# Negated softmax maxima: turned by VectorE's 32x32 blocks and sent by small transfers, in place of TensorE transposes and an addition

## The chip, the cores and the metric

The kernel runs on one NeuronCore of a Trainium2 chip. The metric is device time in microseconds of one execution; lower is better. The core has five engines with instruction queues of their own that run side by side and wait for each other through semaphores: TensorE (PE in the profile; its weight loads are listed as PEld), VectorE (DVE), ScalarE (ACT), GpSimd (POOL) and SyncE (SP), which computes nothing and here issues most of the DMA transfers. SBUF is the on-chip memory of 128 partitions; PSUM holds matmul results in 8 banks.

## The reference

The input is x, 4 sequences of 512 tokens with 256 features, all float32. The computation has four parts:

1. Each sequence goes through one gated feed-forward expert out of 8, chosen by the largest entry of its row of `cond_8`.
2. Attention with 16 query heads of 16 features and a single key and value head:

```
q  = (einsum('bte,oe->bto', x, Wq) + bq) * 16**-0.5
k, v = split(einsum('bte,oe->bto', x, Wkv) + bkv)
qr = q.reshape(bsz, NUM_HEADS * tgt_len, HEAD_DIM)       # 8192 query rows
attn_weights = einsum('brd,bsd->brs', qr, k)
attn_probs   = softmax(attn_weights, axis=-1)
attn_output  = einsum('brs,bsd->brd', attn_probs, v)
```

The reshape is a plain one: each token gives 16 query rows. Then an output projection, and x is added.

3. A linear layer whose weight is a sum of 8 masked matrices, mixed by `cond_8`.
4. A mixture of 8 experts with 2 chosen per token and a capacity of 128 per group, added to the result of part 2.

The change touches the softmax of part 2 only. The softmax needs, for every one of 4 x 8192 query rows, the maximum over 512 keys, subtracted before the exponential.

## The kernel before, in words

**Order of the work.** The order of all instructions is written out by hand (`tc.manual_schedule()`): each engine executes its instructions in the order in which the program names them, and SP issues its transfers in that order too. A framework adds the semaphore waits where data or buffers need them. Three stretches follow each other: the conditional expert for all four sequences (0 to some 108 us of the profile), attention with the linear layer and the routing beside it (to about 395 us), and the experts (to the end).

**Attention, units and steps.** A unit `u` is a quarter of a sequence: `b, hg = divmod(u, 4)`; it has 128 tokens by 16 query rows. There are 16 units. Queries lie in `q`, one tile per sequence, two in turn: `[128 partitions, 4 (i), 512 tokens]`. The partitions are four groups (`j`) of 32; in each group rows 0 to 15 hold the 16 features of a query, and rows 16 to 31 are zero. The keys `k` are laid out likewise, four copies in four groups of 32 rows; rows 16 to 31 of each hold ones. So whatever stands in row 16 of a query (`HD` is 16) is added to all its products with the keys. `projection` makes them: `queries(co)` (L316) multiplies, ScalarE writes `stage`, and 8 transfers per call (L327) copy 16 partitions each into q.

The main loop has 64 steps `n` of the exponentials, 4 per unit, and runs the maxima six steps ahead (`LEAD`), `m = n + 6`:

- `maxima(m, js)` (L379): for a block `i` of the unit and each j, a matmul with 128 query rows as weights and 512 keys as the moving operand (L388) into a PSUM bank ("m", 3 of them; in the lead also "x"), and a VectorE reduction that writes the negated maximum of each row (L392) into `negm`, two tiles that take turns by unit.
- `shifted(u)` (L396): when a unit's maxima are complete, four TensorE transposes (L402) turn its `negm` tile, so that each negated maximum comes to partition 32j + 16 of its query's column; VectorE adds q (L406) and writes `qs`, a copy of the unit's queries with the negated maxima in row 16.
- `exponentials(n, js)` (L412): matmuls with 128 keys as weights and the 512 query columns of `qs` as the moving operand (L420), and ScalarE's exponentials (L421). Since row 16 of the keys is one, the product comes out with the maximum subtracted.
- `weigh(n, js)` (L426): the exponentials times the values (L435); the values have a column of ones, which gives the sums. At the end of a unit the result is copied to `stage` and stored in `od` (L445).
- `side(b, k)`: other work, by a table for the step's place k in its sequence: the next sequence's queries in k = 0 and 1, keys and values in 2 and 3; `values` (k = 2) loads the last sequence's results from `od` (L456, L460), `inverse` (k = 3) takes the reciprocal of the sums on VectorE (L485) and sends it out and back (L486, L490), `normalise` follows in k = 5, then output projection, linear layer (k = 6 to 10) and routing.

A step is called in two halves: maxima of two j, exponentials of two j, then weighing or other work. In the steps with `q`, `k`, `v`, `out`, `rT` or `mix` beside them ("dense") the weighing is all in the second half. After the last maxima (from n = 58 on) the steps have exponentials and weighing only.

`shifted(u)` is called when `m % 4 == 1`, two steps after the maxima of the unit's last block: `turning` in the main loop, and `m == 5` in the lead for unit 0. The unit's exponentials begin in the next step.

Of the kernel before, what the change touches and what calls it, by code (L numbers as in the profile page):

```python
# [10 lines left out]
F32 = mybir.dt.float32  # L11
I32 = mybir.dt.int32
AF = mybir.ActivationFunctionType
ALU = mybir.AluOpType
AX = mybir.AxisListType
PSUM = bass.MemoryType.PSUM

P = 128
# [7 lines left out]
HD = 16  # L26
# [15 lines left out]
def adaln_attn_ffn_kernel(  # L42
# [24 lines left out]
    nc = tc.nc  # L67
    mm = nc.tensor.matmul

    const = ctx.enter_context(tc.tile_pool(name="const", bufs=1))  # L70
# [6 lines left out]
    def bank(tag):  # L77
        return ps.tile([P, 512], F32, tag=tag, name=f"ps_{tag}", bufs=BANKS[tag])
# [14 lines left out]
    nil = const.tile([P, 512], F32, name="nil")  # L93
# [36 lines left out]
    qp = attn_ctx.enter_context(tc.tile_pool(name="qp", bufs=2))  # L130
# [67 lines left out]
    ident = const.tile([P, P], F32, name="ident")  # L198
# [39 lines left out]

    negm = []
    for n in range(2):  # L240
        t = const.tile([P, 4, 4, 32], F32, name=f"negm{n}")
        nc.gpsimd.memset(t, 0.0)
        negm.append(t)

    q_tiles = []
    for n in range(2):
        t = const.tile([P, 4, T], F32, name=f"q{n}")
# [3 lines left out]
    def mixed(b, g):  # L251

        c = cond_sb[:, b, g : g + 1]
        w = w2_sb[:, g, :].rearrange("p (c o) -> p c o", c=2)
        wb = wb_sb[:, b, :, 0:D]
        if g == 0:
            nc.vector.tensor_scalar(wb, w, c, None, ALU.mult)
        else:
            nc.vector.scalar_tensor_tensor(wb, w, c, wb, ALU.mult, ALU.add)
# [37 lines left out]


    seqs = [{} for _ in range(B)]
    qs_of = {}  # L300
    e_of = {}
    pa_of = {}
    scatters, last_rows, weighed = [], [], []
# [7 lines left out]
    def project(b):  # L311

        s = seqs[b]
        s["q"] = q_tiles[b % 2]

        def queries(co):  # L316
            def piece():
                pq = bank("x")
                for c in range(2):
                    mm(pq, wq_sb[:, c, ts(co, P)], coT[:, c, ts(b, T)], start=c == 0, stop=c == 1)  # L320
                qd = qp.tile([P, T], F32, name="stage", bufs=4)
                nc.scalar.activation(
                    qd, pq, AF.Identity, bias=bqs_sb[:, co : co + 1], scale=HD**-0.5
                )
                for n in range(2):
                    for j in range(4):
                        nc.sync.dma_start(  # L327
                            s["q"][32 * j : 32 * j + HD, 2 * co + n, :],
                            qd[ds(64 * n + HD * j, HD), :],
                        )  # L330
            return piece

        def keys():
            s["k"] = qp.tile([P, T], F32, name="k")
            pk = bank("x")
            for c in range(2):
                mm(pk, wk_sb[:, c, :], coT[:, c, ts(b, T)], start=c == 0, stop=c == 1)  # L337
            nc.scalar.activation(s["k"], pk, AF.Identity, bias=bk_sb)

        def values():  # L340
            s["v"] = qp.tile([P, 4, 32], F32, name="v")
            pv = bank("x")
            for sc in range(4):
                for c in range(2):
                    mm(  # L345
                        pv[:, ts(sc, 32)], coT[:, c, ds(b * T + sc * P, P)], wv_sb[:, c, :],
                        start=c == 0, stop=c == 1,
                    )
            nc.vector.tensor_tensor(
                s["v"], pv[:, 0:P].rearrange("p (s d) -> p s d", s=4),  # L350
                bv_sb.unsqueeze(1).to_broadcast([P, 4, 32]), ALU.add,
            )

        return {
            "q0": queries(0), "q1": queries(1), "k": keys, "v": values,
        }
# [22 lines left out]
    def maxima(m, js):  # L379

        u, i = divmod(m, 4)
        b, hg = divmod(u, 4)
        q = seqs[b]["q"]
        k = seqs[b]["k"]
        nm = negm[u % 2]
        for j in js:
            pm = bank("x" if len(js) == 4 and j == 3 else "m")
            mm(  # L388
                pm, q[32 * j : 32 * j + 32, i, ts(hg, P)],
                k[32 * j : 32 * j + 32, :], start=True, stop=True,  # L390
            )
            nc.vector.tensor_reduce(  # L392
                nm[:, i, j, HD : HD + 1], pm, AX.X, ALU.max, negate=True
            )

    def shifted(u):  # L396

        b, hg = divmod(u, 4)
        nm = negm[u % 2]
        pt = bank("x")  # L400
        for i in range(4):
            nc.tensor.transpose(  # L402
                pt[:, ts(i, P)], nm[:, i].rearrange("p j d -> p (j d)"), ident
            )
        qs = qp.tile([P, 512], F32, name="qs")
        nc.vector.tensor_tensor(  # L406
            qs.rearrange("p (i t) -> p i t", i=4), pt.rearrange("p (i t) -> p i t", i=4),
            seqs[b]["q"][:, :, ts(hg, P)], ALU.add,
        )
        qs_of[u] = qs  # L410

    def exponentials(n, js):  # L412
        u, sc = divmod(n, 4)
        k = seqs[u // 4]["k"]
        if n not in e_of:
            e_of[n] = ep.tile([P, 4, 4, P], F32, name="e")
        for n4, j in enumerate(js):
            px = bank("m" if n4 >= 2 else "x")
            rows_j = slice(32 * j, 32 * j + 32)
            mm(px, k[rows_j, ts(sc, P)], qs_of[u][rows_j, :], start=True, stop=True)  # L420
            nc.scalar.activation(  # L421
                e_of[n][:, :, j, :].rearrange("p h (i t) -> p i h t", i=4),
                px.rearrange("p (i h t) -> p i h t", i=4, h=4), AF.Exp,
            )

    def weigh(n, js):  # L426

        u, sc = divmod(n, 4)
        b, hg = divmod(u, 4)
        if u not in pa_of:  # L430
            pa_of[u] = bank("a")
        e = e_of[n]
        j0, nj = js[0], len(js)
        for hh in range(4):
            i = mm(  # L435
                pa_of[u][32 * hh : 32 * hh + 32, j0 * P : (j0 + nj) * P], seqs[b]["v"][:, sc, :],
                e[:, hh, j0 : j0 + nj].rearrange("p j n -> p (j n)"),
                start=sc == 0 and j0 > 0, stop=sc == 3 and j0 == 0,
            )
        weighed.append(i)  # L440
        if sc == 3 and j0 == 0:
            o = qp.tile([P, T], F32, name="stage", bufs=4)

            (nc.vector.tensor_copy if u >= 4 * B - 2 else nc.scalar.copy)(o, pa_of[u])  # L444
            (nc.scalar if u == 4 * B - 1 else nc.sync).dma_start(od[b, hg], o)  # L445
# [325 lines left out]
    STEPS = 16 * B  # L771
# [29 lines left out]
    ]  # L801
    for m in range(LEAD):
        maxima(m, (0, 1, 2, 3))
        if m == 5:
            shifted(0)
        for f, b, k in before_steps[m]:
            f(b, k)
        while mixing:
            mixed(*mixing.pop(0))
# [239 lines left out]
    for n in range(STEPS + 1):  # L1049
        m = n + LEAD  # L1050
        if n in (0, 26, 42, 56):
            residual((0, 26, 42, 56).index(n))
        b, k = divmod(n, 16)
        names = [name for _, name in (last if b == B - 1 else beside)[k]] if b < B else []
        dense = (b == 0 and k in behind) or any(
            name.rstrip("0123") in ON_PE and (b > 0 or name in projection[0]) for name in names
        )
        turning = m <= STEPS + 1 and m % 4 == 1
        if m >= STEPS:
            if n < STEPS:  # L1060
                exponentials(n, (0, 1, 2, 3))
            if turning:
                shifted(m // 4 - 1)
            if n == STEPS:

                up(0, 0)
            weigh(n - 1, (2, 3))
            weigh(n - 1, (0, 1))
            if n < STEPS:
                side(b, k)  # L1070
        elif dense:

            maxima(m, (0, 1))
            exponentials(n, (2, 3))
            if turning:
                shifted(m // 4 - 1)
            side(b, k)
            maxima(m, (2, 3))
            exponentials(n, (0, 1))
            if n > 0:  # L1080
                weigh(n - 1, (2, 3))
                weigh(n - 1, (0, 1))
        else:

            maxima(m, (0, 1))
            exponentials(n, (2, 3))
            if n > 0:
                weigh(n - 1, (2, 3))
            maxima(m, (2, 3))
            exponentials(n, (0, 1))  # L1090
            if turning:
                shifted(m // 4 - 1)
            side(b, k)
            if n > 0:
                weigh(n - 1, (0, 1))

    places = itertools.count()

# [154 lines left out]
```

## Time and profile before

| | us |
|---|---|
| median of three timed runs | 688.33 (687.2 to 688.59) |
| the profiled execution, its own time | 676.98 |
| its span, first to last instruction | 675.3 |
| TensorE busy | 656.4 (97%) |
| VectorE busy | 329.6 (49%) |
| ScalarE busy | 225.8 (33%) |
| maxima, reductions (L392) on VectorE | 160.6 + 4.1 |
| transposes of negm (L402) on TensorE | 10.5 |
| addition of q (L406) on VectorE | 10.9 |
| exponentials (L421) on ScalarE | 132.4 + 6.6 |

A line of groups names the source line, the engine, the operation, output and inputs, their shapes, the count, then busy microseconds and mean nanoseconds of one, and last the engine's idle time just before them, with what ended it. A line of the timeline begins with start and duration in microseconds; several alike are merged (x2). A matmul in float32 is listed as two records. Busy times of TensorE overlap: matmuls on different groups of 32 partitions run side by side, and their ends are modelled. SPq is SP's queue: the window of a transfer there is the time to issue it; its landing is listed apart.

### The profile page before, as it was taken

How to read it: one execution, taken by the hardware profiler on the slowest of the kernel's cores; microseconds unless marked ns; L12 is line 12 of the kernel's file. 1: busy time of each engine (PE TensorE's matmuls, PEld its weight loads, DVE VectorE, ACT ScalarE, POOL GpSimd, SP SyncE). 2: the span in 40 equal slices, each digit the busy share in tenths (PEclk: the TensorE clock that was granted, in tenths of full speed). 3: DMA queues.
4: the chain of work that ended last, by engine and by line, in shares of the span. 5: the costliest groups of instructions: out<-in, count | busy, mean ns of one | idle time of the engine just before them, and what ended most of it. 6: DMA issues, size and time to landing. Idle time of an engine off the chain costs nothing.

```text
span 675.3 us, 10833 instructions
## 1 busy us (share of the span) xinstructions
PE 656.4 (97%) x4106; PEld 406.9 (60%) x4106; DVE 329.6 (49%) x782; ACT 225.8 (33%) x400; POOL 118.0 (17%) x149
## 2 busy tenths in 40 slices
PE   8999999999999999999999999999999999999992
PEld 3444433444344433443335368888999999988881
DVE  1174855666667677766897754264222222221110
ACT  1122114555554555455553651222111111121110
POOL 1710000000000000310013041135332222232331
PEclk9999999999999999999999999999999999999997
DMA  6931992100031101330024199537989999975311
GB/s 215 376 108 28 248 259 66 33 17 17 11 96 56 48 17 54 116 103 17 21 85 166 64 323 336 161 106 232 277 255 329 330 323 317 337 235 153 82 22 26
DMA packets 63483, 102.40 MB, mean 152 GB/s; under 512 B 6464, under 2 KB 26560, under 8 KB 63296
## 3 DMA queue, kind: packets, MB, share of 16 engines
q1 hardware_dynamic: 47536, 81.51, 35.7%
q0 software_dynamic: 7008, 10.56, 7.6%
q10 hardware_dynamic: 8880, 9.57, 5.5%
q8 instruction: 34, 0.56, 0.3%
q14 instruction: 25, 0.20, 0.1%
HBM read 75.37 MB, written 24.15 MB: 147 GB/s over the span
## 4 chain that ended last, share of the span: by engine, by line
PE 92%; DVE 3%; DMA 2%; issue 1%; POOL 0%; ACT 0%; SPq 0%; POOLq 0%; DVEq 0%
PE ps_m L983 19%; PE ps_m L388 19%; PE ps_x L1013 17%; PE ps_a L435 9%; PE ps_a L286 4%; PE ps_x L270 4%; PE ps_x L288 4%; PE ps_x L420 3%; PE ps_x L547 2%; PE ps_x L320 2%; PE ps_x L515 2%; PE ps_x L402 1%; DVE negm L392 1%; PE ps_x L337 1%; PE ps_a L968 1%; PE ps_x L345 1%
## 5 line engine op out<-in xcount | busy, mean ns | idle before, releaser
L392 DVE TENSOR_REDUCE negm<-ps_m 128x1 f32<-128x512 f32 x250 | 160.6, 685 | 73.3 <-PE ps_x L420 60.1
L421 ACT ACTIVATE e<-ps_x 128x512 f32<-128x512 f32 x244 | 132.4, 594 | 119.8 <-PE ps_x L420 115.9
L388 PE MATMUL ps_m<-k,q 32*128 32x512 f32 x500 | 150.4, 639 | 0.1
L420 PE MATMUL ps_x<-qs,k 32*128 32x512 f32 x488 | 139.9, 639 | 0.0
L983 PE MATMUL ps_m<-xT,wi_sb 128*128 128x128 f32 (+1 forms) x800 | 130.3, 321 | 0.0
L1013 PE MATMUL ps_x<-wo_sb,e 128*128 128x256 f32 x576 | 128.5, 379 | 0.0
L983 PEld LDWEIGHTS ps_m<-xT,wi_sb 128*128 128x128 f32 x800 | 119.0, 191 | 10.1 <-issue 0.4
L1013 PEld LDWEIGHTS ps_x<-wo_sb,e 128*128 128x128 f32 x576 | 107.6, 190 | 13.7
L987 ACT ACTIVATE e<-ps_m 128x512 f32<-128x512 f32 x72 | 42.8, 597 | 194.1 <-PE ps_m L983 192.6
L1024 POOL DMA_INDIRECT out_dram<-y,to_row x36 | 56.1, 1558 | 140.5 <-DMA out_dram<-y,to_row 74.4
L388 PEld LDWEIGHTS ps_m<-k,q 32*128 32x128 f32 x500 | 44.6, 183 | 54.3 <-issue 23.9
L435 PE MATMUL ps_a<-e,v 128*32 128x256 f32 x1024 | 73.7, 387 | 1.4 <-ACT stage L444 1.0
L435 PEld LDWEIGHTS ps_a<-e,v 128*32 128x32 f32 x1024 | 24.2, 108 | 70.6 <-issue 54.4
L970 DVE COPY xT<-ps_a 128x256 f32<-128x256 f32 (+1 forms) x23 | 12.2, 529 | 95.1 <-PE ps_a L968 95.1
L1023 DVE TENSOR_SCALAR y<-ps_x,w 128x256 f32<-128x256 f32 x36 | 17.4, 482 | 81.2 <-PE ps_x L1013 81.2
L665 POOL DMA_INDIRECT xp<-x,to_i x32 | 33.2, 1038 | 57.7 <-DVE negm L392 34.1
L420 PEld LDWEIGHTS ps_x<-qs,k 32*128 32x128 f32 x488 | 38.6, 183 | 3.3 <-issue 2.6
L597 POOL TENSOR_SCALAR x<-mk 128x4 f32<-128x4 f32 x4 | 0.8, 210 | 219.6 <-DVE mk L594 219.5
L291 DVE SCALAR_TENSOR_TENSOR hid<-ps_x,wo_sb,sg 128x512 f32<-128x512 f32 x16 | 12.0, 749 | 47.1 <-PE ps_x L288 44.1
L286 PE MATMUL ps_a<-xT_sb,wi_sb 128*128 128x512 f32 x64 | 30.5, 598 | 0.9 <-DMA wi_sb<-in_wcond_dram 0.9
L288 PE MATMUL ps_x<-xT_sb,wi_sb 128*128 128x512 f32 x64 | 30.1, 592 | 0.0
L270 PE MATMUL ps_x<-hid,wo_sb 128*128 128x512 f32 x64 | 28.7, 595 | 0.0
(155 smaller groups left out, 472.6 us busy)
## 6 DMA issues: line engine op xcount, KB each, us to landing
wi_sb<-in_wi_dram SPq DMA_DIRECT2D x25, 1024.0 KB, 8.1
wo_sb<-in_wo_dram SPq DMA_DIRECT2D x25, 1024.0 KB, 8.0
xp<-zeros ACTq DMA_DIRECT2D x1, 8580.0 KB
od<-stage SPq DMA_DIRECT2D x15, 256.0 KB, 2.1
wi_sb<-in_wcond_dram SPq DMA_DIRECT2D x12, 256.0 KB, 5.8
xt<-xp SPq DMA_DIRECT2D x11, 260.0 KB, 5.9
xT_sb<-in_xT_dram SPq DMA_DIRECT2D x4, 512.0 KB, 7.7
w_sb<-in_w_dram SPq DMA_DIRECT2D x8, 256.0 KB, 5.2
```

The source lines that it names most:

```text
L270: mm(po, wd[:, hc, ts(dc, P)], hid_of[b][:, hc, :], start=hc == 0, stop=hc == 3)
L286: mm(pu, wu[:, c, :], xT_sb[:, c, ts(b, T)], start=c == 0, stop=c == 1)
L288: mm(pg, wg[:, c, :], xT_sb[:, c, ts(b, T)], start=c == 0, stop=c == 1)
L388: mm(pm, q[32 * j : 32 * j + 32, i, ts(hg, P)], k[32 * j : 32 * j + 32, :], start=True, stop=True,)
L392: nc.vector.tensor_reduce(nm[:, i, j, HD : HD + 1], pm, AX.X, ALU.max, negate=True)
L420: mm(px, k[rows_j, ts(sc, P)], qs_of[u][rows_j, :], start=True, stop=True)
L421: nc.scalar.activation(e_of[n][:, :, j, :].rearrange("p h (i t) -> p i h t", i=4), px.rearrange("p (i h t) -> p i h t", i=4, h=4), AF.Exp,)
L435: i = mm(pa_of[u][32 * hh : 32 * hh + 32, j0 * P : (j0 + nj) * P], seqs[b]["v"][:, sc, :], e[:, hh, j0 : j0 + nj].rearrange("p j n -> p (j ...
L983: mm(ph[:, ts(k, n)], wi_of[u][:, c, ts(f0 + k, P)], xT_of[u][:, c, :], start=c == 0, stop=c == 1,)
L987: nc.scalar.activation(hT_of[u][:, f0 : f0 + each].rearrange("p f t -> p (f t)"), ph, AF.Gelu_apprx_tanh,)
L1013: mm(po[:, 0:D], hT_of[u][:, fc, ts(h, P)], wo_of[u][:, fc, :], start=fc == 0, stop=fc == F // P - 1,)
L1024: i = nc.gpsimd.indirect_dma_start(out=out_rows, out_offset=bass.IndirectOffsetOnAxis(ap=to, axis=0), in_=y, in_offset=None, compute_op=AL ...
```

## The change

Four edits, all around `shifted`:

- The maxima are kept closer: `negm` becomes `[128, 4 (i), 32]`, with j in the first 4 of 32 columns.
- `shifted(u)` is now one VectorE transpose of 128x128, which turns each block of 32x32 by itself, into `nmT`, and four SP transfers. Each takes 4 partitions (one for each j), for each of them 4 runs (i) of 32 elements, and writes them to row 16 of the four groups of the query tile itself. There is no `qs`; the exponentials read q directly, as 4 runs of 128 columns.
- Row 16 of a query tile then holds old maxima when the tile is used again (sequences 2 and 3). `queries` therefore sends zeros from `nil` into that row first, two more transfers per call.
- `shifted(u)` is called at once after the unit's last maxima: at the end of the step with `m % 4 == 3` (steps n = 1, 5, 9, ...), and at `m == 3` for unit 0. On SP's queue its transfers come behind the query transfers of places 0 and 1 and ahead of the loads of `values` in place 2.

```diff
-        t = const.tile([P, 4, 4, 32], F32, name=f"negm{n}")
+        t = const.tile([P, 4, 32], F32, name=f"negm{n}")
...
                 for n in range(2):
+                    if b > 1:
+                        nc.sync.dma_start(s["q"][HD:P:32, 2 * co + n, :], nil[0:4, :])
                     for j in range(4):
...
-                nm[:, i, j, HD : HD + 1], pm, AX.X, ALU.max, negate=True
+                nm[:, i, j : j + 1], pm, AX.X, ALU.max, negate=True
...
     def shifted(u):
         b, hg = divmod(u, 4)
-        nm = negm[u % 2]
-        pt = bank("x")
-        for i in range(4):
-            nc.tensor.transpose(
-                pt[:, ts(i, P)], nm[:, i].rearrange("p j d -> p (j d)"), ident
-            )
-        qs = qp.tile([P, 512], F32, name="qs")
-        nc.vector.tensor_tensor(
-            qs.rearrange("p (i t) -> p i t", i=4), pt.rearrange("p (i t) -> p i t", i=4),
-            seqs[b]["q"][:, :, ts(hg, P)], ALU.add,
-        )
-        qs_of[u] = qs
+        nmT = qp.tile([P, 4, 32], F32, name="nmT")
+        nc.vector.transpose(
+            nmT.rearrange("p i t -> p (i t)"), negm[u % 2].rearrange("p i j -> p (i j)")
+        )
+        for a in range(4):
+            nc.sync.dma_start(
+                seqs[b]["q"][HD:P:32, :, ds(hg * P + 32 * a, 32)],
+                nmT[32 * a : 32 * a + 4],
+            )
...
-            mm(px, k[rows_j, ts(sc, P)], qs_of[u][rows_j, :], start=True, stop=True)
+            mm(
+                px, k[rows_j, ts(sc, P)], seqs[u // 4]["q"][rows_j, :, ts(u % 4, P)],
+                start=True, stop=True,
+            )
...
-        if m == 5:
+        if m == 3:
             shifted(0)
...
-        turning = m <= STEPS + 1 and m % 4 == 1
...
-            if turning:
-                shifted(m // 4 - 1)
...
+        if m < STEPS and m % 4 == 3:
+            shifted(m // 4)
```

The lines with `turning` stand in all three branches of the main loop and go from each.

More of the change, by code (lines that the diff above doesn't have):

```diff
@@ L299, in adaln_attn_ffn_kernel @@
     seqs = [{} for _ in range(B)]
-    qs_of = {}
     e_of = {}
@@ L1074, in adaln_attn_ffn_kernel @@
             exponentials(n, (2, 3))
-            if turning:
-                shifted(m // 4 - 1)
             side(b, k)
@@ L1090, in adaln_attn_ffn_kernel @@
             exponentials(n, (0, 1))
-            if turning:
-                shifted(m // 4 - 1)
             side(b, k)
```

## The prediction

> **What bounds the kernel now.** I read the page first (busy shares, slices, the chain that ended last), then the groups by shape, then the instruction timeline of the attention stretch (108 to 394 us) and SP's own timeline. The page's chain by engine:
>
> ```profile
> PE 92%; DVE 3%; DMA 2%; issue 1%; POOL 0%; ACT 0%; SPq 0%; POOLq 0%; DVEq 0%
> ```
>
> The groups that the change removes (count, then busy us and mean ns, then idle before):
>
> ```profile
> L406 DVE TENSOR_TENSOR qs<-ps_x,q 128x512 f32<-128x512 f32 x16 | 10.9, 682 | 0.3 <-PE ps_x L402 0.3
> ...
> L402 PE MATMUL ps_x<-ident,negm 128*128 128x128 f32 x64 | 10.5, 286 | 0.0
> ```
>
> TensorE carries the chain, and L402 has 1.4% of it by line: 9.5 us of 675.3. What one turning is worth depends on the step. I call the stretch from one pair of maxima to the next a half step. TensorE's timeline at unit 7 (step 27):
>
> ```profile
> 307.64 0.70 PE L388 MATMUL ps_m<-k,q 32*128 32x512 f32 x2
> ...
> 309.28 0.96 PE L388 MATMUL ps_m<-k,q 32*128 32x512 f32 x2
> ...
> 310.61 0.66 PE L402 MATMUL ps_x<-ident,negm 128*128 128x128 f32 x4
> 311.20 0.64 PE L435 MATMUL ps_a<-e,v 128*32 128x256 f32 x8
> 311.77 1.13 PE L388 MATMUL ps_m<-k,q 32*128 32x512 f32 x4
> ...
> 314.10 0.70 PE L388 MATMUL ps_m<-k,q 32*128 32x512 f32 x2
> ```
>
> Ordinary halves alternate 1.64 and 1.90 us; with the turning they take 2.49 (309.28 to 311.77) and 2.33. So one turning costs 1.28 us here: 0.59 of TensorE, the rest because the 0.68 us addition delays VectorE's maxima, which free the three "m" banks. In steps dense with projections TensorE runs back to back, VectorE idles 0.3 to 0.8 us a half, and a turning costs only its 0.49 us.
>
> SP matters too. Its timeline where queries and attention outputs meet (steps 16 to 19):
>
> ```profile
> 181.41 4.94 SPq L327 DMA_DIRECT2D q<-stage  x8
> 186.45 0.53 SPq L445 DMA_DIRECT2D od<-stage  x1
> 187.07 5.54 SPq L327 DMA_DIRECT2D q<-stage  x8
> 192.67 0.58 SPq L456 DMA_DIRECT2D sum<-od  x1
> 193.30 1.34 SPq L460 DMA_DIRECT2D o<-od  x2
> 197.03 0.33 SPq L486 DMA_DIRECT2D ivd<-iv  x1
> ```
>
> SP is solid from 181.4 to 194.6: about 0.62 us per issue. VectorE's reciprocal of these sums follows, without a wait today:
>
> ```profile
> 196.25 0.29 DVE L349 TENSOR_TENSOR v<-ps_x,bv_sb 128x128 f32<-128x128 f32 x1 [0.43 <-PE ps_x L345]
> 196.46 0.54 DVE L485 RECIPROCAL iv<-sum 128x64 f32<-128x64 f32 x1
> ...
> 197.30 1.29 DVE L392 TENSOR_REDUCE negm<-ps_m 128x1 f32<-128x512 f32 x2 [0.30 <-PE ps_x L420]
> ```
>
> **What the Trainium skill says.** "DMA: Bandwidth & Descriptors", Anatomy of one DMA: a fixed cost of about 2.0 us, mostly completion, whatever the size. The trace agrees: 1.9 us to landing for q<-stage, 2.1 for sum<-od. "Perfetto Trace Analysis", Per-instruction lifecycle: the profiled window of a DMA instruction is sequencer and descriptor generation, not the movement. So the 0.62 us is SP's time, and small size need not make it shorter; the trace has 0.32 to 0.34 us for lone issues and 0.5 to 0.7 back to back. The same page, Identifying Dependency Chains: an instruction waiting on several engines gets EventSemaphore instructions ahead of it. The trace shows them at 51 ns each on TensorE's queue. "VectorE: DVE Perf Modes", The three transpose paths: 311 ns for a 128x128 bf16 turn in 32x32 blocks. No run here shows it.
>
> **Part by part.**
>
> *Removed: 64 transposes, 16 additions.* Units 0 to 3, 5, 6, 9, 10 and 14 fall in dense steps: 9 x 0.49 = 4.4 us. Units 7 and 11: 1.28 each, 2.6. Units 4, 8, 12 and 13 also have other VectorE work around them; there I count 0.58 for the transposes and the excess of the next half (3.40 against 2.99, or 2.00 against 1.64): 0.95 each, 3.8. Unit 15 is priced below as a whole. Gain 10.8 us. One "x" bank per unit falls free too, counted at nothing: it was taken where TensorE waited anyway.
>
> *Added on VectorE: 16 turns.* I take 0.31 us; bounds 0.19 (a 128x32 operation here) and 0.68 (the addition). They come after a step's last maximum, ahead of the next half's reductions, where VectorE waits 0.35 to 0.8 us for TensorE, so nearly all is hidden. Without that cover 16 x 0.31 = 5.0. I take 0.6, for the steps with routing work.
>
> *Waits on TensorE.* The first exponential matmul of each unit waits on four transfers, up to four EventSemaphores: 0 to 0.2 us x 16, so 0 to 3.2. TensorE's queue usually runs ahead, and the maxima that wait on a query transfer and VectorE show no longer half (2.06). I take 0.6. The moving operand becomes four 128-element runs of q; no row shows such a matmul, I count nothing (bounds 0 and a few us).
>
> *Added on SP: 64 transfers of 2 KB, and 8 zero fills for the last two sequences.* Usually SP is idle and they are covered: unit 4's maxima end near 169.6, plus turn and four issues and 1.9 us lands near 174, against exponentials at 176 or later. Three places differ. Let c be SP's time per small issue; I take 0.62, as q<-stage, bounds 0.33 (lone) and 1.1 (the longest q<-stage is 1139 ns).
>
> Unit 5 (step 17) and unit 9 (step 33). The turned maxima are queued behind both query sets, and the sums behind them. The first zero fill issues early, since it waits only for old exponentials; three fills and four turned transfers remain ahead of sum<-od: 7c. In unit 5 the sums land at 192.67 + 2.1 + 7c. The reciprocal could start at 196.05 (end of v, 0.49 earlier than before). VectorE is in order: behind the reciprocal wait the maxima of the next two positions, behind these the "m" banks and TensorE. About 0.6 us of slack (0.30 idle before the reductions, some 0.3 until the bank is asked for) comes off: 7c - 1.9 = 2.5 us. In unit 9 sum<-od issued at 267.43 and v ended at 272.61: 7c - 3.2 = 1.1. The exponentials, which need the turned maxima by about 197.7 in unit 5, are hidden behind this stall or late by less. Unit 1 also comes after 16 query transfers (they end at 122.38), but lands by 125.7 against 127.1, no loss.
>
> Unit 15 (step 57). The following steps have no maxima and are short, and in VectorE's queue the turn stands behind the last sequence's first ranking, which ends with L595 at 380.34. Turn 0.31, semaphore 0.1, so first issue at 380.75, last at + 3c, landing 1.9 later: 384.5. TensorE's exponentials of step 60 start today at 383.44:
>
> ```profile
> 380.15 0.19 DVE L595 TENSOR_TENSOR hot<-rev,mk 128x32 f32<-128x32 f32 x1
> ...
> 381.26 0.66 PE L402 MATMUL ps_x<-ident,negm 128*128 128x128 f32 x4
> ...
> 383.44 0.70 PE L420 MATMUL ps_x<-qs,k 32*128 32x512 f32 x2
> ```
>
> So a loss of 3c - 0.8 = 1.1 us, its own saved transposes included.
>
> *Smaller negm fills* on POOL are early and hidden. From 395 us on TensorE runs the experts without a break (265.00 busy of 265 in that window), and their loads and rows follow the earlier work, so the gain passes to the end.
>
> Sum: -10.8 + 0.6 + 0.6 + 2.5 + 1.1 + 1.1 = -4.9 us. The profiled execution would go from 676.98 to 672.1. The timed median is 688.33, 11.4 above it, a difference that the profile doesn't explain; I carry the same 4.9 over: **683.4 us**.
>
> **Rivals.**
>
> *Full cover.* SP issues these tiny transfers in 0.33 us. Unit 5 then loses 0.4, unit 9 nothing, unit 15 0.2: -10.8 + 1.2 + 0.6 = -9.0, 679.3 us. For it: lone issues take that. Against: everything back to back takes 0.5 or more.
>
> *Slower: SP becomes the bound in steps 16 to 19 and 32 to 35 and at unit 15.* Each transfer has 16 runs of 128 bytes; if c is 1.1, the three places lose 5.8, 4.5 and 2.5, and -9.6 + 12.8 = +3.2: 691.5 us. It decides above c = 0.91 (17c = 9.6 + 1.9 + 3.2 + 0.8). For it: the longest query issue; against: their median, 587 ns.
>
> *Landing late everywhere.* If four runs of 128 bytes per partition landed 2 to 3 us later than the 1.9 of the query transfers, the spare of ordinary units would be gone and fifteen exponentials would wait; 0.5 us each takes 7.5 us and gives about 691 once the three places grow as well. Nothing in the profile says so: DMA engines are under 30% busy there, and 32 KB lands in 1.9.
>
> *Hardly any gain:* the hidden waits on TensorE (3.2) or VectorE (5.0) show in full: 686 to 687.
>
> **How the numbers follow.** Forecast 0.52; full cover 0.17; hardly any gain 0.12; slow SP 0.12; late landing 0.07. A change of this kernel can be told from none at about 0.2%, 1.4 us. Faster: 0.52 + 0.17 and half of "hardly any", 0.75; same 0.08; slower 0.17. The range 678.8 to 690.2 leaves out the ends of full cover and of both slow cases. The likeliest case alone: 681 to 686.
>
> **What would show it.** Halves at 311.77 and its like back to 1.64 and 1.90; no L402 or L406. SP solid from the query transfers to sum<-od, 4.3 us later than before relative to the first of them, and VectorE idle before the reciprocal in steps 19 and 35, released by a DMA. TensorE idle about 1 us before step 60, released by the q transfers. I am wrong if small issues take clearly other than 0.62 us, if other exponentials wait on q transfers, or if exponential matmuls last longer than 0.59 to 0.70 us.

## The result, and the profile after

| | before, us | after, us | ratio, 95% interval |
|---|---|---|---|
| first measurement | 688.31 | 692.19 | 1.0065 (1.0048 to 1.0082) |
| chip 12, later | 677.46 | 673.14 | 0.9935 (0.9918 to 0.9951) |
| chip 0, later | 687.68 | 692.25 | 1.0060 (1.0039 to 1.0080) |

The measurement that the prediction was made for says 0.65% slower, and 692.2 lies outside the forecast's range. The other two rows came with the experiments: the chips on which these kernels ran fall into two kinds. On chips 9, 12 and 13 the kernel before takes 677.5 to 677.6 us, on chips 0 and 11 (and in the first measurement) 687.2 to 688.3, each time within a few tenths of a per cent. I call these the shorter and the longer level. Only chip 0 was met twice, both times at the longer level, so the runs don't tell the chip from the time at which it ran. The profile of before that the prediction was made from (676.98 us) is of the shorter level, the times beside it are of the longer one.

Of the profile after, first the chain by engine:

```profile
PE 87%; DVE 3%; DMA 3%; SPq 2%; another core or an unknown queue 1%; ACT 1%; issue 1%; POOL 0%; POOLq 0%; DVEq 0%
```

TensorE still carries it, but with 87% in place of 92%. New are SP's queue and a releaser that the profile cannot name. L402 and L406 are gone; in their place stands (count, then busy us and mean ns, then idle before):

```profile
L403 DVE STREAM_TRANSPOSE nmT<-negm 128x128 f32<-128x128 f32 x16 | 4.9, 306 | 0.4
```

TensorE's timeline at unit 7, where the prediction showed halves of 1.64, 2.49 and 2.33 us (start, duration, count at the end):

```profile
311.13 0.70 PE L391 MATMUL ps_m<-k,q 32*128 32x512 f32 x2
...
312.77 0.96 PE L391 MATMUL ps_m<-k,q 32*128 32x512 f32 x2
...
314.67 0.70 PE L391 MATMUL ps_m<-k,q 32*128 32x512 f32 x2
...
316.52 0.74 PE L391 MATMUL ps_m<-k,q 32*128 32x512 f32 x2
```

They are 1.64, 1.90 and 1.85 now: the gain is there. Next SP's timeline and what waits for it in unit 5:

```profile
188.35 3.33 SPq L330 DMA_DIRECT2D q<-stage  x4
191.79 2.40 SPq L407 DMA_DIRECT2D q<-nmT  x4
194.23 0.56 SPq L459 DMA_DIRECT2D sum<-od  x1
```

```profile
196.41 0.55 DVE L488 RECIPROCAL iv<-sum 128x64 f32<-128x64 f32 x1 [3.15 <-DMA sum<-od]
196.88 2.53 DVE L395 TENSOR_REDUCE negm<-ps_m 128x1 f32<-128x512 f32 x4
197.56 0.69 PE L391 MATMUL ps_m<-k,q 32*128 32x512 f32 x1 [1.50 <-DVE negm L395]
```

The four transfers stand ahead of the sums, at 0.60 us each; the reciprocal waits 3.15 us for the sums, the maxima stand behind it, and TensorE waits for the banks that these free. That is the step which the prediction priced at 2.5 us. What it did not price comes next. In this view of windows, PEclk is the third value from the end:

```profile
197.00:199.00 2.00, 1.44 (x10) 0.67 (x14) 1.98 (x4) 0.10 (x1) 0.00 (x0) 1.00 0.53 193
199.00:201.00 2.00, 2.00 (x16) 0.52 (x8) 0.41 (x1) 0.99 (x2) 0.00 (x0) 0.57 0.16 53
201.00:203.00 2.00, 2.00 (x16) 0.58 (x16) 1.29 (x2) 1.34 (x3) 0.00 (x0) 0.58 0.31 104
```

For some 3.4 us after the stall TensorE runs at half its clock, and the next half takes 3.03 us for 1.90.

Three more stalls, near 291, 363 and 396 us, had no place in the prediction at all. The timeline of all engines at the first:

```profile
289.18 0.97 POOL L668 DMA_INDIRECT xp<-x,to_i  x1 [0.30 <-issue]
289.66 1.12 PE L391 MATMUL ps_m<-k,q 32*128 32x512 f32 x2
291.82 1.29 DVE L395 TENSOR_REDUCE negm<-ps_m 128x1 f32<-128x512 f32 x2 [4.77 <-PE ps_m L391]
291.96 1.08 ACT L424 ACTIVATE e<-ps_x 128x512 f32<-128x512 f32 x2 [3.91 <-PE ps_m L391]
292.56 0.69 PE L391 MATMUL ps_m<-k,q 32*128 32x512 f32 x1 [1.78 <-DVE negm L395]
```

VectorE and ScalarE stand still for 4 to 5 us while GpSimd issues the last two of eight indirect scatters of routed rows (L668); TensorE runs on until it needs a bank, and then waits for VectorE. VectorE's wait is put down to a matmul of TensorE that ended 4.0 us before (why it was not seen earlier is taken up below, where the scatters are moved); in the same stretch at the shorter level VectorE never idles over 0.8 us (timeline below). The half that begins at 289.66 takes 5.73 us, where it takes 2.07 at the shorter level.

### The profile page after: what moved, and what is told of

Read it like the earlier page. It is cut to its first block, busy times and chain, and to the rows that moved or that the text cites. A ratio compares the mean times of both kernels' runs of the same rounds, so it can differ in the third digit from the quotient of the medians.

```text
span 690.5 us, 10751 instructions
## 1 busy us (share of the span) xinstructions
PE 660.7 (96%) x4042; PEld 403.1 (58%) x4042; DVE 324.0 (47%) x782; ACT 226.0 (33%) x400; POOL 116.1 (17%) x149
## 4 chain that ended last, share of the span: by engine, by line
PE 87%; DVE 3%; DMA 3%; SPq 2%; another core or an unknown queue 1%; ACT 1%; issue 1%; POOL 0%; POOLq 0%; DVEq 0%
PE ps_m L986 18%; PE ps_m L391 18%; PE ps_x L1016 17%; PE ps_a L438 8%; PE ps_a L287 4%; PE ps_x L271 4%; PE ps_x L289 4%; PE ps_x L550 2%; PE ps_x L320 2%; PE ps_x L518 2%; PE ps_x L420 2%; DVE negm L395 2%; PE ps_a L971 1%; SPq L407 1%
## 5 line engine op out<-in xcount | busy, mean ns | idle before, releaser
L391 PE MATMUL ps_m<-k,q 32*128 32x512 f32 x500 | 157.2, 651 | 5.6 <-DVE negm L395 5.5
L420 PE MATMUL ps_x<-q,k 32*128 32x512 f32 x488 | 143.6, 654 | 3.5 <-DVE xT L973 2.2
L986 PE MATMUL ps_m<-xT,wi_sb 128*128 128x128 f32 (+1 forms) x800 | 131.7, 323 | 0.0
L391 PEld LDWEIGHTS ps_m<-k,q 32*128 32x128 f32 x500 | 46.4, 186 | 63.5 <-DVE negm L395 35.5
L438 PE MATMUL ps_a<-e,v 128*32 128x256 f32 x1024 | 76.3, 395 | 3.1 <-issue 2.0
L420 PEld LDWEIGHTS ps_x<-q,k 32*128 32x128 f32 x488 | 38.7, 186 | 7.7 <-issue 4.4
L668 POOL DMA_INDIRECT xp<-x,to_i x32 | 32.1, 1004 | 57.2 <-DVE negm L395 34.3
L1024 POOL CAST to_row<-at 128x1 int32<-128x1 f32 x36 | 19.8, 551 | 66.0 <-DVE at L1009 66.0
```

Of the source, the lines that this page charges most:

```text
L391: mm(pm, q[32 * j : 32 * j + 32, i, ts(hg, P)], k[32 * j : 32 * j + 32, :], start=True, stop=True,)
L420: mm(px, k[rows_j, ts(sc, P)], seqs[u // 4]["q"][rows_j, :, ts(u % 4, P)], start=True, stop=True,)
L438: i = mm(pa_of[u][32 * hh : 32 * hh + 32, j0 * P : (j0 + nj) * P], seqs[b]["v"][:, sc, :], e[:, hh, j0 : j0 + nj].rearrange("p j n -> p (j ...
L668: i = nc.gpsimd.indirect_dma_start(out=xp, out_offset=bass.IndirectOffsetOnAxis(ap=to_i[:, k, ch : ch + 1], axis=0), in_=s["x3"][:, ch, 0: ...
L986: mm(ph[:, ts(k, n)], wi_of[u][:, c, ts(f0 + k, P)], xT_of[u][:, c, :], start=c == 0, stop=c == 1,)
```

## Experiments

Halves are counted as in the prediction, from one pair of maxima to the next. All runs stand beside the kernel before on the same chip.

**The two kernels again (chip 12, shorter level).**

> The kernel before, unchanged, for a second profile of it. Theory A (the 677.0 us profile of before is an execution without stalls, and a usual one holds about 11 us of them): timed 688.3, ratio 1.000, and this profile shows about 688 with stretches of all compute engines idle for 2 to 7 us, each followed by some 3 to 10 us of TensorE at a clock of 0.5. Rival B (the 11 us lie outside what the profile sees, or come from the profiling): a profile at 677 again, TensorE clock 0.994 again, and 688.3 timed.

> The changed kernel again: 692.2 timed. If the three long stalls of its first profile (at 291, 363 and 395 us, about 5, 4 and 12 us with the half clock behind them) belong to the program, they come back at the same instructions, and the profile is again near 692. If they are chance, they are elsewhere or gone, and the profile differs from 692 by several us.

Before: 677.36 us, ratio 0.9999 (0.9990 to 1.0008). After: 673.14, 0.9935 (0.9918 to 0.9951). The profile of after at the place of the first long stall:

```profile
290.55 0.70 PE L391 MATMUL ps_m<-k,q 32*128 32x512 f32 x2
...
291.70 1.29 DVE L395 TENSOR_REDUCE negm<-ps_m 128x1 f32<-128x512 f32 x2 [0.63 <-PE ps_x L420]
...
292.62 0.70 PE L391 MATMUL ps_m<-k,q 32*128 32x512 f32 x2
```

A half of 2.07 us, with scatters in flight up to 291; the stalls near 363 and 396 are gone as well. The stall of unit 5 is there (halves of 5.10 and 2.43 us). So the sum of the prediction holds where its profile was taken: 677.4 to 673.1 is 4.3 us of the 4.9 forecast. Theory A (before's profile was untypical for its place) and rival B (the profile sees nothing) both miss: it is typical, for this level.

**SP's queue: sums ahead of the turned maxima.**

```diff
-        if m < STEPS and m % 4 == 3:
+        if m < STEPS and m % 4 == 3 and m // 4 not in (5, 9):
             shifted(m // 4)
+        if m in (24, 40):
+            shifted(m // 4 - 1)
```

> The changed kernel, but units 5 and 9 are turned and sent one step later, behind the loads of the attention sums on SP's queue. Theory A: the stalls at the reciprocal of steps 19 and 35 go, 3.0 of 4.0 us and 1.0 of 1.2 (three zero fills stay ahead of the sums): 692.2 - 4.0 = 688.2. Rival D (the exponentials of these units, which then wait for transfers that start about 4 us later, take over the wait): 691 to 692.

675.99 us (chip 12), 0.9970 of before (0.9957 to 0.9983), 2.9 us slower than the changed kernel. That is rival D, and worse than it said:

```profile
192.73 1.29 SPq L463 DMA_DIRECT2D o<-od  x2
194.13 2.35 SPq L407 DMA_DIRECT2D q<-nmT  x4
194.27 0.55 DVE L488 RECIPROCAL iv<-sum 128x64 f32<-128x64 f32 x1 [0.69 <-DMA sum<-od]
...
198.97 2.07 PE L420 MATMUL ps_x<-q,k 32*128 32x512 f32 x4 [2.42 <-DMA q<-nmT]
```

The reciprocal's wait falls to 0.69 us, and TensorE waits 2.42 us for the transfers instead. Both waits come of what stands ahead on the queue: the 16 query transfers, and here also the two loads of o, 256 KB each, which the edit puts ahead of the turned maxima. From 194.1 to 197.0 us the DMA engines move 226 packets, only 8 of them under 512 bytes; the 64 packets of 128 bytes that are the turned maxima move from 197.0 to 198.0. The clock is then halved for 6.8 us.

**The changed kernel, without transfers, and with SP's queue relieved (chip 0, longer level).** The second kernel leaves out transfers and fills, so its exponentials have no shift (they are scaled by 0.004 to stay finite). The third:

```diff
     beside = [
...
-        [(1, "q1"), (-2, "rank1")],
+        [(1, "v"), (-2, "rank1")],
         [(-1, "values"), (1, "k"), (-2, "places"), (-2, "rows")],
-        [(1, "v"), (-1, "inv")],
+        [(-1, "inv"), (1, "q1")],
...
             exponentials(n, (0, 1))
+            if m == STEPS - 1:
+                shifted(m // 4)
             side(b, k)
...
-        if m < STEPS and m % 4 == 3:
+        if m < STEPS - 1 and m % 4 == 3:
             shifted(m // 4)
```

> The changed kernel once more, beside the kernel before in the same call, since the first measurement (before 688.3, after 692.2) and the second (before 677.5, after 673.1) differ. Theory E (what decides is where the kernels run: on some chips or at some times both hold extra stalls): the kernel before is either near 677.5 and the changed one near 673, or near 688 and 692, and in the second case the profile shows long stalls while GpSimd issues its indirect scatters. Rival F (chance in each execution): values of one call are spread over both levels.

> The changed kernel without the 64 transfers and the 8 zero fills, VectorE's turns kept; so that the exponentials stay finite without their shift they are scaled by 0.004, and the values that come out are others, so that the routing differs. If the transfers cost only what units 5, 9 and 15 show (5.10+2.43 against 1.64+1.90 us, then 3.38+1.64 against 2.07+1.64, and 4.77 against about 3.35), this runs 4.0 + 1.3 + 1.4 = 6.7 us below the changed kernel: 666.4 where that takes 673.1. If the transfers slow anything else (DMA queues, instruction fetches), it is lower still, or the long stalls of the first measurement go with them.

> The changed kernel with the second half of the query projection and the value projection of the next sequence exchanged (queries in the fourth step instead of the second), so that only 8 query transfers stand ahead of the turned maxima of units 1, 5 and 9 and of the attention sums, and with unit 15 turned and sent ahead of the last routing instead of behind it. My theory (SP's queue makes the stalls): units 5, 9 and 15 lose at most 0.3 us each, and it runs near 666.5 to 667.5 where the changed kernel takes 673.1, 1.5% under the kernel before. Rival (the stalls move to the query transfers, which now stand behind the reciprocal and its round trip): 670 or more.

Before 687.68; after 692.25, 1.0060 (1.0039 to 1.0080): the first measurement repeats, with its stalls at the same halves (7.11 and 3.66 us, 5.75 and 3.34, 5.48), as theory E has it. Without transfers 677.87, 0.9853; with the queue relieved 681.19, 0.9887 (0.9839 to 0.9934). Both still have long stalls (a half of 7.26 us at the second set in the latter), so their totals mix two things, and the totals named in the expectations, for the shorter level, aren't tested. Up to the half where unit 9's reciprocal comes, no scatter is in play; from the first maxima (72 us) to there, the kernel before takes 195.9 us, after 192.2 here (194.5 on chip 12), relieved 190.5, without transfers 190.1. So with the queue relieved the transfers cost 0.4 us up to there, and the rest is unit 5. The relieved kernel at units 5 and 15:

```profile
195.12 0.70 PE L391 MATMUL ps_m<-k,q 32*128 32x512 f32 x2
...
196.79 0.92 PE L391 MATMUL ps_m<-k,q 32*128 32x512 f32 x2
...
377.20 0.31 DVE L403 STREAM_TRANSPOSE nmT<-negm 128x128 f32<-128x128 f32 x1
377.59 2.41 SPq L407 DMA_DIRECT2D q<-nmT  x4
...
382.22 0.70 PE L420 MATMUL ps_x<-q,k 32*128 32x512 f32 x2
```

Halves of 1.67 and 1.87 us in unit 5; in unit 15 the half ahead of step 60 is 3.53 (3.94 before, 4.76 after). The part of my theory that concerns SP is shown.

**Spreading the scatters, first try (chip 9, then chip 0).** The scatters were moved to later steps in the order in which the program is written:

```diff
-            for ch in range(4):
-                for k in range(2):
-                    i = nc.gpsimd.indirect_dma_start(
+                bursts = ((1,) * 8, (3, 3, 2), (2, 2, 2, 2), (8,))[b]
...
+    for part in range(1, 8):
+        beside[4 + part].append((-2, f"scatter{part}"))
```

> The kernel before, for a profile where it takes near 688 (if this call meets that level; at 677 it repeats the earlier profile). Theory G (where a kernel takes the longer time, VectorE and ScalarE stand still while GpSimd issues its indirect scatters of routed rows, until the last scatter of a set of eight is through; each such stall of TensorE is followed by 3 to 10 us at half its clock): the 10 to 11 us of before lie in the same three sets, in halves that begin near 291, 360 and 390 us. Rival H (the extra time of before lies elsewhere, and the stalls at the scatters belong to the changed kernel): these halves are as in its first profile (2.07, 2.54 and 2.08 us).

> The changed kernel with its indirect scatters spread out: the first sequence's eight go one to a step over eight steps, the second's as three, three and two over three steps, the third's as four pairs over four steps, in place of eight in a row each. Theory G: where the changed kernel takes 692 (19 us above its 673), a stall lasts only while one short burst is in flight, and most of the 19 us go: 674 to 682; where it takes 673, nothing changes, 672.5 to 674. Rival (the stalls don't hang on the scatters, but on the place in the program): 690 to 693, with the long halves near 288, 361 and 393 us as before.

> The same spread scatters together with the exchanged projections and the early turn of unit 15 (681.2 without the spread where before took 687.7). Theory G: 667 to 674 at the longer level, 666 to 667 at the shorter. Rival: 681 at the longer level.

Chip 9 has the shorter level: before 677.47 (0.9999), after with this edit 673.97, 0.9936 (0.9915 to 0.9957), and with the queue relieved 668.61, 0.9869 (0.9852 to 0.9885).

> Again for a profile of the kernel before at its longer level, which the third call (677.6) did not meet. Theory G (VectorE and ScalarE stand still while a set of eight indirect scatters is in flight, and TensorE's clock halves after each): its 10 to 11 us lie in the halves near 291, 361 and 390 us. Rival H: these are 2.07, 2.54 and 2.08 us as in its first profile, and the time is elsewhere. If the call meets the shorter level: 677.5 and nothing new.

> Changed kernel with spread scatters, at the longer level if the call meets it. Theory G: 674 to 682 (against 692.2 for the changed kernel there). Rival (the place in the program decides): 690 to 693. At the shorter level it repeats 674.0.

> Exchanged projections, early turn of unit 15 and spread scatters, at the longer level if the call meets it. Theory G: 667 to 674 (681.2 without the spread). Rival: 681. At the shorter level it repeats 668.6.

Chip 0, longer level: 687.42 (1.0005), 689.48 (1.0050, 1.0029 to 1.0072), 682.12 (0.9909, 0.9879 to 0.9939). The spread runs seem to speak for the place in the program, but the trace shows that nothing was spread: GpSimd has no other work between, is bound to no step, and issues its eight scatters 1.28 us apart as ever. The edit tested nothing.

The profile of before at the longer level is worth more. Its span is 685.8 us against 675.6 on chip 12. Summed over the halves around each set of scatters, it loses 1.8 us at the first set, 1.1 at the second and, from there into the experts (to 440 us), 7.2 at the third: 10.1 of these 10.2. Rival H falls: the extra time of before lies at the scatters too. The third set, windows of chip 12 and then of chip 0 (PE busy, PEld, DVE, ACT, POOL, PEclk, DMA share, GB/s):

```profile
396.00:400.00 4.00, 4.00 (x33) 2.85 (x32) 0.97 (x2) 2.37 (x3) 2.18 (x3) 1.00 1.05 406
400.00:404.00 4.00, 4.00 (x20) 3.52 (x20) 3.58 (x2) 1.19 (x2) 0.00 (x0) 1.00 1.04 407
```

```profile
396.00:400.00 4.00, 1.63 (x4) 0.29 (x2) 0.28 (x1) 1.75 (x3) 3.02 (x4) 0.94 0.88 335
400.00:404.00 4.00, 3.78 (x18) 1.48 (x19) 0.00 (x0) 1.58 (x5) 0.95 (x1) 0.50 1.04 410
```

On chip 0 TensorE is busy 1.63 us of four while GpSimd issues three scatters and starts another, and then has half its clock. The same count for the changed kernel (chip 0 against chip 12) gives 6.3 us at the first set, 3.4 at the second and 11.0 at the third; it reaches the first set 2.8 us earlier there, 2.2 of it because unit 5 cost less, and 6.3 + 3.4 + 11.0 - 2.8 = 17.9, the whole difference of the spans (690.5 and 672.6).

**Do the stalls follow the scatters? (chip 11, longer level).** One kernel holds the first set back to step 42. The other truly spreads it, one scatter a step, each waiting for TensorE; its second and third sets, though bound to steps, still went out nearly in a row, since they were late already. Both add to the scatters:

```diff
+                    tc.add_manual_dep(
+                        i.ins, weighed[-1].ins.name, AFTER, reason="not at once"
+                    )
```

> The changed kernel with the first sequence's eight scatters held back from step 36 to step 42 (each waits for TensorE's last weighing of that step), the other sets as they are. Theory G, at the longer level: the halves near 288 us, where the changed kernel lost 5.0 and 1.5 us, are clean (3.0, 2.1, 2.1 us), and either the time falls to about 686 or a stall comes up where the scatters now are, near 305 to 318 us. Rival I (the place in the program decides, scatters or not): the halves near 288 us stay at 5 to 7 us, and 690 to 693. At the shorter level: 673, nothing to see.

> The changed kernel with its scatters truly spread: the first spread edit only moved them in the order in which the program is written, and GpSimd, which has nothing between them, still issued them in a row. Here each burst waits for TensorE's last weighing of its step: one a step over eight steps, then three, three and two over three, then four pairs. Theory G, at the longer level: a stall lasts at most until one short burst is through, 674 to 684. Rival I: 689 to 693. At the shorter level: 673 to 674.

> The truly spread scatters with the exchanged projections and the early turn of unit 15. Theory G, at the longer level: 667 to 675 (681 and 682 without true spreading). Rival I: 680 to 684. At the shorter level: 667 to 669.

Before 687.89; moved 697.62, 1.0135 (1.0118 to 1.0151); spread 682.24, 0.9911 (0.9893 to 0.9929); spread and relieved 677.94, 0.9853 (0.9830 to 0.9875). With the set moved, the halves near 290 us are clean (2.07, 2.13, 2.36), and the timeline has this where the scatters now are:

```profile
308.87 1.12 PE L391 MATMUL ps_m<-k,q 32*128 32x512 f32 x2
...
312.12 0.97 POOL L675 DMA_INDIRECT xp<-x,to_i  x1 [0.31 <-issue]
314.92 1.89 DVE L395 TENSOR_REDUCE negm<-ps_m 128x1 f32<-128x512 f32 x3 [7.32 <-remote]
315.07 1.08 ACT L424 ACTIVATE e<-ps_x 128x512 f32<-128x512 f32 x2 [7.58 <-remote]
315.67 1.22 PE L391 MATMUL ps_m<-k,q 32*128 32x512 f32 x1 [5.68 <-DVE negm L395]
```

The half at 308.87 takes 9.82 us for 1.90. The stall follows the scatters: rival I falls. VectorE comes back 2.80 us after GpSimd began the last of the eight, as it does in the other profiles: 2.64 in the first profile after, 2.59 on chip 0, 1.96 in before.

What is late is a signal. VectorE's maxima and ScalarE's exponentials wait for one semaphore, which TensorE raises when matmuls end, and the trace keeps a record of each update. In the changed kernel on chip 0, eight matmuls that raise it end between 284.80 and 288.84 us. No update is recorded from 283.92 to 289.78 us, and then eight within 0.33 us; VectorE starts at 289.85 and ScalarE at 289.99. On chip 12 each update of that stretch follows the end of its matmul within 0.15 us, and in none of the ten profiles of the shorter level does one come more than 0.6 us late. So TensorE's signals don't arrive while the row of scatters is in flight, and the two engines that wait for them stand still. ("remote" in the lines above names an update for which the view finds no instruction that ended shortly before.) Some records are missing in the traces of the longer level (849 of 860 for this semaphore on chip 0), but in the first set all eight are there. What holds the signals up isn't shown. The packets of the scatters themselves aren't slower: in the first set they take 123 ns each, on the mean, on chip 0 and on chip 12.

With the set spread (three in a row, then 4.5 to 6.8 us apart) the halves near 291 are clean too (2.08, 2.13, 2.36), while the second set, in a row, costs a half of 7.78 us. So the row stalls; scatters 4.5 us or more apart did not.

**All three sets handed out singly (met the shorter level, chip 13).** One scatter at each step or weighing, the experts' first loads two steps later for it:

```diff
         weighed.append(i)
+        if held and (n < 48 and j0 == 0 or n >= 48):
+            f, nth = held.pop(0)
+            f(nth)
...
-        [(-1, "rT0"), (-1, "rT1"), (0, "pairs1")],
+        [(-1, "rT0"), (-1, "rT1")],
...
-        [(-1, "choose"), (-1, "rank0")],
+        [(0, "pairs1"), (-1, "choose"), (-1, "rank0")],
```

> The kernel before with the scatters of the first three sequences handed to GpSimd one at a time, each waiting for a weighing of TensorE: the first set one a step, the second and third one at each weighing (about 2 us apart); the first weights of the experts are loaded two steps later for it. If rows of scatters make the stalls, then at the longer level this falls from 688 by most of the 10 to 11 us: 677 to 682. Rival (2 us apart is as bad as 1.3): the first set's 1.6 us go, the rest stays: 686. At the shorter level 677 to 678.

> The same handing out in the changed kernel. If rows of scatters make its 19 us of stalls: 673 to 678 at the longer level, 4 us under the kernel before with the same edit, as the sum and the shorter level have it. Rival: 682 as with the first spreading, the second and third sets still stalling. At the shorter level 673.

> The same handing out, with the exchanged projections and the early turn of unit 15: 667 to 672 at the longer level (rival: 676 to 678, as with the first spreading), 667 to 669 at the shorter.

680.20 (1.0036, 1.0026 to 1.0047), 676.13 (0.9980, 0.9964 to 0.9996) and 671.98 (0.9916, 0.9900 to 0.9933), beside 677.58. The edit itself costs 2 to 3.4 us there (the half ahead of step 60 grows from 3.94 to 8.82 in before, from 4.77 to 7.87 in after); between the two kernels the 4.1 us stay. What it does at the longer level wasn't met.

## Why the prediction was wrong

**The step that failed** is the one from profile to time: "The timed median is 688.33, 11.4 above it, a difference that the profile doesn't explain; I carry the same 4.9 over". The profile was of the shorter level, where the sum is nearly right (4.3 for 4.9 us). The 11 us are stalls at three sets of scatters (10.1 of the 10.2 us that the profiles of before differ by), and they do not carry over: in the changed kernel they are 20.7, or 10.6 more, of which 2.8 come back ahead of the first set. In the four profiled executions, 3.0 us won at the shorter level (675.6 to 672.6) become 4.7 lost at the longer one (685.8 to 690.5); in the medians, 4.3 won become 3.9 and 4.6 lost. I had seen the gap, and named it as unexplained; what follows from an unexplained 11 us in a forecast of 5 is that it can change with the kernel, which was none of my rivals.

Why the changed kernel loses more is partly seen. The stall ends with its set, so its length is set by where in the set VectorE and ScalarE run out of signals. In before, at the first set, VectorE comes to a stop 0.4 us after the last scatter began; in the changed kernel (chip 0) 2.2 us ahead of it, with two still to come, and in the moved set 4.5 us ahead of it. What decides that point isn't shown. Late instruction fetches could be thought of: in the changed kernel on chip 0 no packet of an instruction queue moves between 282.7 and 294 us, around a stop from 285.1 to 289.9. But the fetch that comes at 294.2 us there comes at 291.0 on chip 12, where that stretch is reached 2.8 us later. It is late by 6.0 us, about what the stall costs, so it can be a result of the stall as well as a cause.

**Removed work: right.** 9.6 us of gain net of turns and waits were forecast outside units 5, 9 and 15. In the halves of chip 12, leaving out those of units 5, 9 and 15 and the stretches around the first two sets, it is 8.4; those stretches (0.4 and 0.6) and unit 9's own transposes (0.4) bring it to 9.8. A dense unit gained 0.39 to 0.44 for the 0.49 forecast, unit 7 1.07 for 1.28. The turn took 0.31 us, what the Trainium skill ("VectorE: DVE Perf Modes", The three transpose paths) has for elements of half the size, and exponential matmuls kept 0.59 to 0.70 us with their moving operand in four runs.

**Issue time c: right.** 0.54 to 0.60 us for 0.62; the fills 0.54.

**Unit 5: right in mechanism, one term missing.** Priced 2.5, measured 1.9 and 2.2 (chip 0), 3.1 (chip 9), 4.1 (chips 12 and 13), 4.0 (first profile), 4.3 and 5.5 (chip 11). Two things make the spread. The reciprocal waits 2.2 us where no query transfer takes over 0.9 us to issue (chips 0 and 9), and 2.9 to 3.2 us where one of them takes 1.4 to 1.5. And on chip 0 there is no half clock behind the stall, elsewhere there is, for 3.4 us (6.8 in the case of 5.5), which the prediction has no term for. "TensorE: Matmul & The Clock Gate" in the skill (Part 1) has windows of 3413 ns that run free, and half rate after an idle one; the length agrees. Windows that run free could also let like stalls end differently: the reciprocal waits 2.18 us on chip 0 and 2.19 on chip 9, and only the second halves the clock. But TensorE idled 0.5 to 1.5 us in these stalls, far less than a whole window, so what halves the clock here stays open.

**Unit 9: right** (1.1 forecast; 1.3 in the first profile, 1.6 on chip 12, the transposes that it saves left out). **Unit 15: half.** 1.1 forecast; the half ahead of step 60 grew by 0.83, and the half after next fell by 0.28, 0.5 in all.

**Landing: right.** On chip 12 only one exponential of the changed kernel waits for turned maxima, that of unit 15, for 1.34 us, and the wait ends 1.74 us after the last of the four transfers began to issue (priced 1.9). The rival that has them land late everywhere falls. One figure of the prediction is off by its own terms, without effect: unit 1's maxima would land at 122.38 + 3 x 0.62 + 1.9 = 126.1 us, not 125.7, still ahead of 127.1.

**The slow rival (691.5 for c above 0.91)** came out near the measured time by accident: c is 0.60.

## What to carry to other kernels

A profile bears only on times of its own level: when its execution lies 11 us from the median, find where these 11 us are before a sum of 5 is carried over, and take the profile and the times of both kernels on one chip. A queue that issues in order (SP here) makes a tiny transfer cost what stands before it: exchanging two projections (with unit 15's early turn) was worth 4.2 to 5.4 us at the shorter level, as much as the change itself or more, and 4.3 to 11 at the longer one, where the stalls change too. The kernel so relieved beats both kernels on chips 0 and 9 (0.989 to 0.991 and 0.987 of before). On some chips, eight indirect transfers in a row from GpSimd can hold up engines that have nothing to do with them; 4.5 us apart or more they did not.

## What the runs showed that I had not expected

- On two chips of five a row of eight indirect scatters, 1.28 us apart, can keep TensorE's signals from VectorE and ScalarE, which then stand still for up to 9.3 us, until 2.0 to 2.8 us after the last one began; on three chips the same program runs through.
- A stall of TensorE by 0.5 to 2.4 us can be followed by 3.4 or 6.8 us at half clock: at unit 5 the same wait cost 1.9 us without it and 3.1 with it.
- Moving an instruction later in the program text delays nothing on an engine that has no other work before it; only a wait does.
